# Two half terms of k side by side behind an up and a down pass

## The chip, the cores and the metric

The kernel runs on one core of one Trainium2 chip. The metric is the device time of one execution in microseconds (us), the median of several runs. All arithmetic is in float32.

## The reference, cut to what matters

A batch of 8 images with 512 channels and 32 x 32 positions goes through four layers, image by image except for the routing of the last:

```python
# layer 0: group norm, 8 heads of attention, three inner steps, projection, residual
q, k, v = split(qkv_w @ group_norm(x) + qkv_b)
h = softmax(q.T @ k / 8) @ v
for _ in range(3):
    h = h + 0.1 * tanh(inl_w @ h + inl_b)
x = x + proj_w @ h + proj_b
# layer 1: one attention over the 1024 positions, with 64 channels for q and k, residual
x = v1 @ softmax(q1.T @ k1).T + x
# layer 2: 12-tap filters, twice as fine along both axes, leaky relu, back to 32 x 32
x = down2(leaky_relu(up2(x + bias), 0.2) * sqrt(2))
# layer 3: per image, weights mixed from 8 experts by a router, 1x1, 3x3, 1x1, residual
w1, w2, w3 = (sum(gate[e] * w[e] for e in range(8)) for w in (W1, W2, W3))
out = relu(bn3(w3 @ relu(bn2(conv3x3(w2, relu(bn1(w1 @ x)))))) + x)
```

## The kernel before

Channels or positions lie on the 128 partitions of SBUF. Large products (q, k, v, inner steps, projection, and the weighting of layer 1) are done by Strassen's scheme in Winograd's form: seven half-sized products instead of eight, named P1, C11, U2, U3, C22, C21 and C12, and gathered by additions on VectorE as the PSUM banks are evacuated. Expert weights of layer 3 are mixed for seven images together (`blend_early`) and for the last one by itself.

The work is a loop over the 8 images: `layer0`, `layer1`, then `between` for images 0 to 6, or `last_across`, `last_rows` and `last_columns` for image 7, after which layer 3 of all images follows. `between(b)` holds layer 2 of image b together with q, k and v of image b + 1, so that TensorE has work while layer 2 waits for its evacuations and its trips through DRAM.

Layer 2 applies filters as small matmuls. `wide` filters along one axis, its result is written to DRAM (`across`) and read back turned (`turned`). Then come the vertical passes, in eight steps n (two halves e of the channels, four steps i each):

- `up(e, i)` (L1178): 8 matmuls, each shown as 2 records, in TensorE tiles of 32 x 64 (L1188), into two pairs of PSUM banks from `ps_sc`, which has just these two. ScalarE writes 0.2 times each pair to a tile `fine` (L1194), VectorE takes the maximum of the two (L1195).
- `down(e, i)` (L1197): 8 matmuls, shown as 16 records, in tiles of 64 x 32 (L1206) over `fine`, into two banks of `ps_tp`; two copies into a tile `sent` (L1212), on ScalarE, or one of them on VectorE in odd steps; four stores of `sent` to DRAM (`back_u`, L1215). `sent` has two buffers.
- `turn_back(e)` (L1219), after the fourth step of a half: two loads that bring the half back turned (L1224). After the passes `narrow` (L1226) filters what they bring.

`fine_passes` (L1260) writes the order out: round n issues up(n), a filling, down(n - 1) and another filling, for n from 0 to 8 (no down in round 0, no up in round 8). In images 0 to 6 one filling is the next of the 14 half terms of k, two halves of each of the seven products (`in_turn`, L577: 4 records of 128 x 128 matmuls at L607, in banks of `ps_mm`, which has two). Its evacuation is one instruction: on ScalarE for P1 and C11 (L624, L626), on VectorE for the others (L628, L635). In image 7 (`last_rows`, L1351) one filling is two of the 34 pieces of `blend_early` (L291): one matmul each (L297), a copy to a tile `mix` of four buffers, by ScalarE for odd and VectorE for even pieces (L301), and a store to DRAM from POOL's queue (L302). The third and sixth fillings also load the 2 MB of images 0 and 1 for layer 3 (`load_z`, L1382); after every seventh piece follows a load of further experts (L288).

Inside these parts TensorE, VectorE, ScalarE and SP run in the order of the program (`hand`, L1274: `tc.manual_schedule`); POOL's order is made by the scheduler. So is what crosses from one hand-written part to the next: SP has the first two loads of image 0's mixed weights (L1442) ahead of the last `turn_back`.

Of the kernel before, what the change touches and what calls it, by code (L numbers as in the profile page):

```python
# [54 lines left out]
def tile_sequence(ctx: ExitStack, tc: tile.TileContext, a: dict, out: bass.AP, shifted: bool):  # L55
# [1084 lines left out]
    class Layer2:  # L1140
# [119 lines left out]
        def fine_passes(self, fill=lambda: None):  # L1260
            order = [(e, i) for e in range(2) for i in range(4)]
            for n in range(len(order) + 1):
                if n < len(order):
                    self.up(*order[n])
                fill()
                if n:
                    e, i = order[n - 1]
                    self.down(e, i)
                    if i == 3:
                        self.turn_back(e)  # L1270
                fill()

    engines = mybir.EngineType
# [409 lines left out]
```

## Time and profile before

| what | value |
|---|---|
| median of 3 runs | 3649.24 us (3649.09 to 3654.0) |
| profiled execution, device time | 3648.9 us |
| its span, first to last instruction | 3647.0 us |
| granted TensorE clock | 0.998 of full speed |
| TensorE, VectorE, ScalarE busy | 3572.2, 2406.2, 1329.7 us |
| up passes, 1024 records (L1188) | 587 to 639 ns each, several at once |
| down passes, 1024 records (L1206) | 589 to 613 ns each, several at once |
| stores of mixed weights (L302), to landing | 3.0 / 6.4 / 10.0 us min / median / max |
| stores of `sent` (L1215), to landing | 2.3 us median |
| loads of `turn_back` (L1224), to landing | 7.6 us median |

Lines of the page group instructions by their line in the source, engine and tiles; "x" is a count. PE is TensorE's matmul, PEld its weight load, DVE is VectorE, ACT ScalarE, SP and POOL the engines whose queues issue the transfers (SPq, POOLq and so on are the queues themselves). The chain is the work that ended last, followed back from the end of the program. A wait reads "who waited <- for whom: us in total, times, longest". Where several matmuls run at the same time in different tiles, their records overlap, and only the distance from the start of one block to that of the next tells what the block costs.

### The profile page before, as it was taken

Reading aid. Unit: us, or ns where it says so; the run is one execution under the profiler, and the core shown is the slowest. Engines: PE = TensorE matmul, PEld = TensorE weight load, DVE = VectorE, ACT = ScalarE, POOL = GpSimd, SP = SyncE. Lnnn points to the kernel's source line nnn. Section 1 sums busy time; section 2 is a strip of 40 time slices with the busy share of each in tenths; the row PEclk is TensorE's granted clock in tenths of the full one; section 3 lists DMA queues with packets and bytes.
Section 4 is the critical chain, followed back from the end, with each engine's and each line's share of the span. In section 5 each row is a group of like instructions: output and inputs, shape, how many; then the busy total and the mean of one; then the engine's idle time right before and its main releaser. Section 6 shows DMA issues by size and latency. Waiting matters only on the chain.

```text
span 3647.0 us, 47655 instructions
## 1 busy us (share of the span) xinstructions
PE 3572.2 (98%) x19445; PEld 1751.4 (48%) x19445; DVE 2406.2 (66%) x3201; ACT 1329.7 (36%) x1772; POOL 102.0 (3%) x139
## 2 busy tenths in 40 slices
PE   8999999999999999999999999999999999999799
PEld 4346543474435643474435743465434744355243
DVE  4887568765777558765687658774687657765434
ACT  0632345223542246223452236323452235422343
POOL 4100000000000000000000000000000000001100
PEclk9999999999999999999999999999999999999999
DMA  5102440116101450015301351024401261015872
GB/s 200 50 1 84 130 162 1 45 65 198 69 1 64 133 179 1 32 53 170 122 1 64 97 174 42 1 84 130 162 1 46 66 201 64 1 43 190 311 272 108
DMA packets 139813, 348.24 MB, mean 95 GB/s; under 512 B 14720, under 2 KB 89488, under 8 KB 132800
## 3 DMA queue, kind: packets, MB, share of 16 engines
q1 hardware_dynamic: 135120, 325.96, 26.0%
q0 software_dynamic: 4320, 18.87, 1.4%
q8 instruction: 155, 2.54, 0.3%
q14 instruction: 74, 0.61, 0.1%
q10 hardware_dynamic: 144, 0.26, 0.0%
HBM read 226.55 MB, written 118.49 MB: 95 GB/s over the span
## 4 chain that ended last, share of the span: by engine, by line
PE 94%; DMA 2%; issue 1%; ACT 1%; DVE 1%; POOL 0%; SPq 0%; POOLq 0%; ACTq 0%; DVEq 0%
PE scores L827 12%; PE av L868 12%; PE inl_X L552 7%; PE inl_A L552 5%; PE av_X L1129 5%; PE inl_Y L552 5%; PE av_A L1129 3%; PE av_Y L1129 3%; PE v_X L552 3%; PE c L1497 2%; PE proj_X L552 2%; PE v_X L607 2%; PE k_X L607 2%; PE v_Y L552 2%; PE av L881 2%; PE q_X L607 2%
## 5 line engine op out<-in xcount | busy, mean ns | idle before, releaser
L846 ACT ACTIVATE e<-scores 128x1024 f32<-128x1024 f32 x504 | 516.6, 1025 | 434.4 <-PE scores L827 379.3
L827 PE MATMUL scores<-q,k 64*64 64x512 f32 x4096 | 531.9, 592 | 0.0
L868 PE MATMUL av<-e,v 64*64 64x512 f32 x4096 | 528.7, 589 | 0.0
L852 DVE TENSOR_TENSOR acc<-acc,e 128x1024 f32<-128x1024 f32 x320 | 389.3, 1217 | 37.4 <-ACT e L846 35.4
L868 PEld LDWEIGHTS av<-e,v 64*64 64x64 f32 x4096 | 156.6, 133 | 282.8 <-issue 276.8
L827 PEld LDWEIGHTS scores<-q,k 64*64 64x64 f32 x4096 | 150.4, 133 | 295.5 <-issue 220.8
L552 PE MATMUL inl_X<-T_hf,w_inl 128*128 128x512 f32 x576 | 261.6, 592 | 0.0
L1195 DVE TENSOR_TENSOR fine<-up,fine 128x1024 f32<-128x1024 f32 x128 | 150.8, 1220 | 118.8 <-ACT fine L1194 116.5
L889 DVE RECIPROCAL inv<-av 128x256 f32<-128x256 f32 x128 | 223.1, 1748 | 2.1 <-PE av L881 2.1
L692 ACT ACTIVATE inl_U<-inl_U,inl_b 128x512 f32<-128x512 f32 x96 | 66.8, 719 | 304.4 <-DVE inl_U L707 304.4
L552 PEld LDWEIGHTS inl_X<-T_hf,w_inl 128*128 128x128 f32 x576 | 108.8, 190 | 137.9 <-issue 111.7
L552 PE MATMUL inl_A<-hf,w_inl 128*128 128x512 f32 x384 | 174.6, 597 | 0.0
L1194 ACT ACTIVATE fine<-up 128x1024 f32<-128x1024 f32 x128 | 124.1, 1022 | 134.1 <-PE up L1188 121.1
L850 DVE TENSOR_TENSOR acc<-e,e 128x1024 f32<-128x1024 f32 x64 | 79.3, 1240 | 111.3 <-ACT e L846 92.3
L703 DVE TENSOR_TENSOR inl_U<-inl_X,inl_P 128x512 f32<-128x512 f32 x96 | 61.8, 685 | 109.9 <-PE inl_X L552 109.9
L1129 PE MATMUL av_A<-v,eT 128*128 128x256 f32 x512 | 122.6, 383 | 0.0
L552 PEld LDWEIGHTS inl_A<-hf,w_inl 128*128 128x128 f32 x384 | 71.5, 190 | 96.8 <-issue 86.3
L1129 PE MATMUL av_X<-v,eT 128*128 128x256 f32 x512 | 114.0, 381 | 0.0
L1016 ACT ACTIVATE eT<-scores 128x512 f32<-128x512 f32 x128 | 66.1, 602 | 115.4 <-PE scores L379 115.4
L1129 PEld LDWEIGHTS av_X<-v,eT 128*128 128x128 f32 x512 | 96.6, 190 | 19.3 <-DVE av_U L1103 6.5
L1166 ACT COPY wide<-wide 128x1024 f32<-128x1024 f32 x62 | 59.8, 1015 | 122.4 <-PE wide L1158 122.4
L1036 POOL TENSOR_TENSOR seen<-seen,acc 128x512 f32<-128x512 f32 x16 | 20.3, 1269 | 3006.6 <-DVE acc L1028 3006.0
(377 smaller groups left out, 5562.2 us busy)
## 6 DMA issues: line engine op xcount, KB each, us to landing
x<-in_x_dram SPq DMA_DIRECT2D x64, 512.0 KB, 9.3
across_u<-wide SPq DMA_DIRECT2D x128, 256.0 KB, 3.7
turned<-across_u SPq DMA_DIRECT2D x64, 512.0 KB, 5.9
back_u<-sent SPq DMA_DIRECT2D x256, 128.0 KB, 2.3
back<-back_u SPq DMA_DIRECT2D x32, 1024.0 KB, 7.6
w_v<-stored_u_v SPq DMA_DIRECT2D x14, 1792.0 KB, 7.4
out_dram<-z SPq DMA_DIRECT2D x31, 512.0 KB, 2.8
spill_u<-z SPq DMA_DIRECT2D x28, 512.0 KB, 5.9
```

The lines of the kernel that those rows point to most:

```text
L552: nc.tensor.matmul(dst, lhs, rhs, start=(opens and s == 0 and cc == 0), stop=(cc == 1 and s == rows), skip_group_check=True,)
L607: nc.tensor.matmul(dst, lhs, rhs, start=(what in opens and s == 0 and cc == 0), stop=(cc == 1 and s == rows), skip_group_check=True,)
L827: nc.tensor.matmul(ps[r][rows[c]], k[rows[r], oc, jc * P + c * HD : jc * P + c * HD + HD], q[rows[r], oc, ts(sh, HALF)], start=True, stop= ...
L846: nc.scalar.activation(e, pair, AF.Exp, scale=HD ** -0.5)
L850: nc.vector.tensor_add(accs[g], exps[t - 1], e)
L852: nc.vector.tensor_add(accs[g], accs[g], e)
L868: nc.tensor.matmul(avs[g][r][rows[c]], v[rows[r], jc, ts(2 * oc + c, HD)], e[rows[r], ts(c, HALF)], start=(jc == 0), stop=(jc == SC - 1),)
L881: nc.tensor.matmul(ps[rows[r]], ones[:, 0:HD], acc[:, ts(r, HALF)], start=True, stop=True)
L889: nc.vector.reciprocal(copies[g][:, at], totals[g][:, at])
L1129: nc.tensor.matmul(ps[:, ts(s, QR)], left[:, j, at : at + P], right[:, j, :], start=(what in ("P1", "U2", "C22") and s == 0 and j == 0), s ...
L1194: nc.scalar.mul(t, ps, 0.2)
L1195: nc.vector.tensor_max(t, ps, t)
```

## The change

In each round of `fine_passes` the first filling moves from before the down pass to behind it. Round n is then up(n), down(n - 1), with the turn back after every fourth step, and two fillings.

```diff
             for n in range(len(order) + 1):
                 if n < len(order):
                     self.up(*order[n])
-                fill()
                 if n:
                     e, i = order[n - 1]
                     self.down(e, i)
                     if i == 3:
                         self.turn_back(e)
+                fill()
                 fill()
```

No instruction is added or removed. In images 0 to 6 TensorE's queue in round 1 was up, C11, down, U3 and becomes up, down, C11, U3, and likewise in the rounds to 6; the copies of a down pass now stand ahead of both evacuations of k on ScalarE and VectorE. Rounds 0, 7 and 8 keep their order, since there is no down pass in the first and no half term left in the last two.

In image 7 the four pieces of a round follow the down pass together. The last two of the 34 pieces come in round 8, and so stand behind the last down pass instead of ahead of it. On SP the stores of down pass 0 go ahead of the load of image 0 (L1382), and those of down pass 2 ahead of the last load of experts (L288); all else keeps its place. On POOL the two stores change places within four pairs of pieces (4 and 5, 12 and 13, 20 and 21, 28 and 29).

## Prediction

> **What bounds the kernel now.** I read the page's busy row and chain first, to learn which engine's time is the kernel's time.
>
> ```profile
> PE 3572.2 (98%) x19445; PEld 1751.4 (48%) x19445; DVE 2406.2 (66%) x3201; ACT 1329.7 (36%) x1772; POOL 102.0 (3%) x139
> ...
> PE 94%; DMA 2%; issue 1%; ACT 1%; DVE 1%; POOL 0%; SPq 0%; POOLq 0%; ACTq 0%; DVEq 0%
> ```
>
> TensorE is busy for 98% of the span and carries 94% of the chain, so a microsecond taken out of its queue is a microsecond of the kernel, except where it waits. The change touches eight stretches: one per image. The chain in order of time for image 1 (start, length, what) shows such a stretch:
>
> ```profile
> 849.87 1.04 PE up L1188 x16
> 850.92 1.91 PE k_A L607 x4
> 852.83 1.72 PE k_X L607 x4
> 854.55 1.06 PE up L1188 x16
> 855.61 1.91 PE k_A L607 x4
> 857.52 1.02 PE dn L1206 x16
> 858.54 1.91 PE k_X L607 x4
> 860.46 1.04 PE up L1188 x16
> ...
> 889.92 1.04 PE up L1188 x16
> 890.96 1.11 PE dn L1206 x16
> 892.08 0.76 ACT fine L1194
> ```
>
> Three things are to be seen. There is no gap between up at 849.87 and up at 889.92: TensorE sets the pace. A half term of k costs 1.91 us directly behind an up or down pass, but 1.72 us behind another half term (850.92 and 852.83). And the last up is followed directly by a down pass, which begins 1.04 us after it, exactly as a half term does: the new neighbourhood already occurs once per image.
>
> The timeline gives the evacuation of the up pass (start, length, engine, what):
>
> ```profile
> 891.03 1.94 ACT L1194 ACTIVATE fine<-up 128x1024 f32<-128x1024 f32 x2 [2.31 <-PE up L1188]
> 892.09 2.36 DVE L1195 TENSOR_TENSOR fine<-up,fine 128x1024 f32<-128x1024 f32 x2 [1.38 <-ACT fine L1194]
> ```
>
> From up's start at 889.85 in that view to the end of the maximum at 892.09 + 2.36 = 894.45 it is 4.60 us; the next up can't begin earlier, since both pairs of PSUM banks are then taken.
>
> Image 7 differs: its filling is the mixing of the experts. The sums by stretch (second one) and its waits say what bounds it:
>
> ```profile
> 3342.00:3412.00 70.00, 51.77 (x324) 13.29 (x324) 31.55 (x37) 30.29 (x44) 17.89 (x34) 1.00 0.95 345
> ```
>
> ```profile
> ACT mix L301 <- DMA mixed_u<-mix: 22.5, 8, 3.8
> ...
> ACT sent L1212 <- DMA back_u<-sent: 7.8, 3, 3.4
> PE narrow L1237 <- DMA back<-back_u: 7.1, 2, 5.9
> ```
>
> The last two columns of the first are the DMA share and GB/s: 0.95 and 345. TensorE is busy 51.8 of 70 us there; the transfers are the bound.
>
> [...] Up works in 32x64 tiles, down in 64x32 and k in 128x128, [...] the trace agrees that seams cost (1.91 against 1.72), and prices up to down no higher than up to k (1.04 both). [...] the extra 0.19 us is the size of one 128x128 load (190 ns on the profile's page), which fits a load left bare at the seam, though nothing shows that it is the cause. [...]
>
> **The change, part by part.** Each call of the passes makes nine rounds.
>
> *Images 0 to 6, TensorE.* Before, rounds 1 to 6 are up, k, down, k: 1.04 + 1.91 + 1.02 + 1.91 = 5.88 us (in the chain 29.46 us for the five rounds from up at 860.46 to up at 889.92, 5.89 each). After, they are up, down, k, k: 1.04 + 1.02 + 1.91 + 1.72 = 5.69 us. The saving is 0.19 to 0.20 us a round; I take 0.195. Round 0 has no down pass and keeps its order. Rounds 7 and 8 have none of the 14 half terms left (2 + 6 x 2 = 14) and keep theirs. So 6 x 0.195 = 1.17 us an image, 7 x 1.17 = 8.2 us in all. Bounds: 42 x 0.19 = 8.0 and 42 x 0.20 = 8.4. After the passes come v and the next image's attention, where TensorE is again without gaps, so the time isn't given back.
>
> *What moves with a down pass, and its cover.* Each brings 8 matmuls (16 records), two copies of 0.59 to 0.69 us on ScalarE and VectorE, and four stores on SP; every fourth also the two loads of the turn back. (1) Down waits for the maximum of the up before: done at 4.60 us into a round, while the next up begins at 5.69: cover 1.09 us, before 1.29. It is needed by up anyway, so this adds no wait. (2) The copies now stand ahead of both k evacuations on ScalarE and VectorE, not between them. Per round VectorE has at most 2.36 + 0.68 + 0.75 + 0.75 = 4.54 us of work and ScalarE 1.94 + 1.18 + 0.69 = 3.81, both under 5.69. The first k of a round ends at 3.97 us; behind maximum and copy its evacuation ends near 4.60 + 0.68 + 0.75 = 6.0, 0.3 us into the next round, and the earliest half term that needs it or its bank starts 2.06 us in. Nothing, with 1.7 us to spare; if the cover went, the k behind would wait for the shortfall. (3) The stores leave earlier in their round; the two buffers of sent give each two rounds to land, now 11.4 instead of 11.8 us. The median landing is 2.3 us; only dn4's stores, queued behind a turn back of 7.6 us, come near. They cost nothing as long as sent6's copy, behind two activations in round 7, finishes before the maximum of up7 ends. I take 0; a microsecond late would cost up to 1 us an image, and is the upper bound's reason.
>
> *The end of the passes.* Up7, down6, down7 run as before, waiting for up7's evacuation; that stall of some 3.5 us an image stays.
>
> *Image 7.* After, a round is up, down, then four pieces of mixing. Seams save at most 0.2 us a round, and are hidden by the transfers: 0. SP: the stores of down 0 now precede the 2 MB load of z0, and those of down 2 precede the last experts' load; same bytes in the same queue, so what is queued behind all of them (down 3's stores, then the turn back, then down 4's) lands within about 0.5 us of before. POOL: within some pairs of pieces the stores swap places, 0.53 us each. ScalarE: the copies of a down pass stand ahead of both mixing copies. Where they wait for their buffer (7.8 us in three waits), two mixing copies and the next round's L1194 are queued behind them, instead of one. In round 7 that delays piece 29, and pieces 32 and 33 now follow down 7 on TensorE instead of preceding it. Down 7 itself is held by sent6, which waits for down 4's stores, so it stays near 3411. The first weights' load needs piece 32 and stands ahead of the turn back on SP: piece 32 is a down pass and a copy later, 1.02 + 0.69 = 1.7 us; I let 0.5 of it show, since the turn back waits for down 7's own stores anyway, which land some 6.8 us after down 7 begins (3411.13 to 3417.91). That is 0.5 us worse against about 0.5 better from the stores that go ahead: net 0. Bounds -3 (three waits on sent shortened to half) and +4 (piece 29 waits as long as the longest such wait, 3.8).
>
> *Sum.* Against the profiled execution (3648.9 us, span 3647.0 and 1.9 around it): 3648.9 - 8.2 + 0 = 3640.7. The median of the runs, 3649.24, is 0.3 higher: 3641.0.
>
> **The rivals.**
> A, forecast: seams saved, image 7 within its bounds of -3 and +4: 3638 to 3645. Chance 0.72.
> B, image 7's transfers also get better: the waits on sent (7.8 us) all go, because stores go ahead of 2 MB loads, and half of this reaches the end: 8.2 + 3.9 = 12.1, 3637.1. For it: those waits exist. Against: 0.95 DMA share. Chance 0.1.
> C, slower: in image 7 four mixing copies in a row must each find their buffer's last store landed. A store takes a median of 6.4 and up to 10.0 us; if the evacuation of up (4.6), the two mixing copies in ScalarE's queue and that landing run in series rather than beside each other, rounds grow from 8.2 to about 10 us, seven times 1.8 = 12.6, net +4.4: 3653.6. It decides from a growth of 8.2 / 7 = 1.2 us a round. Against: one buffer's loop, a landing plus about 1 us, already sets the round today. Chance 0.06, and 0.07 for a smaller growth that leaves 3645 to 3649.
> D, the change doesn't save: the seam from up to down costs more where k would have followed, or evacuation sets the round at 5.89: 3649. Against: the direct seam at 890.96 and 1.09 us of cover. Chance 0.05.
>
> **How the numbers follow.** The likeliest is A, 3641.0. Leaving out most of B's far side, C and D, 3637.5 to 3645.5 holds some 8 in 10. Changes under 0.2% (7.3 us, about what a measurement of this kernel can tell from none) count as the same: the border is 3641.9, inside A. A lies below it with 0.7 of its chance: 0.5, and B's 0.1: 0.6 faster. C's far part beyond 3656.5 gives 0.03 slower; the rest, 0.37, is the same.
>
> **What would show it.** Right: in the chain, up at 1.04, dn at 1.02, k at 1.91, k at 1.72, and 5.69 us from up to up in rounds 1 to 6; about 46.4 instead of 47.6 us from the first up to the first v of images 0 to 6; image 7's first up to its second narrow pass of half 1 unchanged within 4 us. Wrong: a wait of PE up on DVE fine, a k term waiting for L628 or L635, dn above 1.1 us behind up, or rounds of image 7 above 9 us.

## The result and the profile after

| | before | after |
|---|---|---|
| median of 9 runs each, side by side | 3652.08 us (3649.09 to 3656.84) | 3643.37 us (3639.71 to 3647.46) |
| profiled execution, device time | 3648.9 us | 3643.3 us |
| its span | 3647.0 us | 3641.3 us |
| first up to first narrow, images 0 to 6 | 46.49 us | 45.31 us |
| first narrow to the next image's scores | 32.65 us | 32.65 us |
| first up of image 7 to first product of layer 3 (`c`) | 91.7 us | 94.4 us |

The ratio is 0.9977, with an interval of 0.9967 to 0.9988: faster by 0.23%, just beyond the 0.2% that the prediction set as its border, with that border inside the interval. The forecast was 3641.0 us, the measurement 3643.37.

The page's busy row and chain of the kernel after. The chain is still TensorE's. Its busy time, with the same 19445 records, is only 1.8 us less: it fell by 8.4 us between the first up of image 0 and the first up of image 7, and rose by 7.3 us from there on, where image 7's stretches at a granted clock of 0.50 or 0.51 add up to 30.7 us instead of 10.2.

```profile
PE 3570.4 (98%) x19445; PEld 1757.2 (48%) x19445; DVE 2405.3 (66%) x3201; ACT 1325.9 (36%) x1772; POOL 101.9 (3%) x139
...
PE 95%; DMA 2%; issue 1%; ACT 1%; DVE 1%; POOL 0%; SPq 0%; POOLq 0%; DVEq 0%; ACTq 0%
```

The chain in order of time of the kernel after, image 1 (start, length, what):

```profile
853.08 1.06 PE up L1188 x16
854.14 1.02 PE dn L1206 x16
855.16 1.91 PE k_A L607 x4
857.08 1.72 PE k_X L607 x4
858.79 1.04 PE up L1188 x16
```

From up at 853.08 to up at 858.79 it is 5.71 us, where it was 5.91 (854.55 to 860.46); the rounds that follow take 5.69 or 5.70, without a gap. The second k costs 1.72 us. Six rounds and seven images of this are the whole gain: 7 x (46.49 - 45.31) = 8.3 us, beside 8.7 us between the medians, whose interval runs from 4 to 12 us. What follows the passes is not touched (32.65 us in both).

The end of the evacuation of up7, the last of image 1, in the timeline of the kernel after (start, length, engine, what):

```profile
889.44 2.35 DVE L1195 TENSOR_TENSOR fine<-up,fine 128x1024 f32<-128x1024 f32 x2 [1.39 <-ACT fine L1194]
```

Up7 starts at 887.20 there, so it is evacuated after 889.44 + 2.35 - 887.20 = 4.59 us, as before. In the six rounds ahead of it no matmul waits for an evacuation.

The weight loads of round 1 of image 1 in the same timeline (start, length, then, in brackets, the idle time of the weight loader) show where a seam lies:

```profile
855.09 0.30 PEld L607 LDWEIGHTS k_A<-x,w_k 128*128 128x128 f32 x2 [0.84 <-issue]
855.63 0.19 PEld L607 LDWEIGHTS k_A<-x,w_k 128*128 128x128 f32 x1 [0.24 <-issue]
...
857.77 0.19 PEld L607 LDWEIGHTS k_X<-T_h,w_k 128*128 128x128 f32 x1 [0.24 <-issue]
858.72 0.23 PEld L1188 LDWEIGHTS up<-turned,up_v 32*64 32x64 f32 x16 [0.76 <-issue]
```

Inside the pair a load follows the last by 0.43 us (856.06, 856.49, 856.92). Into the pair it takes 855.63 - 855.09 = 0.54, 0.11 more than 0.43, and out of it 858.72 - 857.77 = 0.95 for two matmuls, 0.09 more than twice 0.43. So a stay in 128x128 tiles costs about 0.11 going in and 0.09 coming out, 0.20 in all, with two k terms inside; before the change a round with two stays of one k term each took 5.91 us, 0.20 more than the 5.71 here. Of the two stays in a round one is left.

### The profile page after: what moved, and what is told of

It is laid out like the page before. It is cut to its first block, busy times and chain, and to the rows that moved or that the text cites. A ratio compares the mean times of both kernels' runs of the same rounds, so it can differ in the third digit from the quotient of the medians.

```text
span 3641.3 us, 47652 instructions
## 1 busy us (share of the span) xinstructions
PE 3570.4 (98%) x19445; PEld 1757.2 (48%) x19445; DVE 2405.3 (66%) x3201; ACT 1325.9 (36%) x1772; POOL 101.9 (3%) x139
## 4 chain that ended last, share of the span: by engine, by line
PE 95%; DMA 2%; issue 1%; ACT 1%; DVE 1%; POOL 0%; SPq 0%; POOLq 0%; DVEq 0%; ACTq 0%
PE scores L827 12%; PE av L868 12%; PE inl_X L552 7%; PE inl_A L552 5%; PE av_X L1129 5%; PE inl_Y L552 5%; PE av_A L1129 3%; PE av_Y L1129 3%; PE v_X L552 3%; PE c L1497 2%; PE proj_X L552 2%; PE v_X L607 2%; PE k_X L607 2%; PE v_Y L552 2%; PE av L881 2%; PE q_X L607 2%
```

## The experiments

All are compared with the kernel before, run beside them on the same chip. `fine_passes` gets an argument `split`: `True` is the order of before (up, k, down, k), and without it the order is that of the change.

**Images 0 to 6 alone, and image 7 alone.** The change touches two kinds of stretch; each was made without the other.

```diff
-            two.fine_passes(fill)                                # last_rows, image 7
+            two.fine_passes(fill, split=True)
```

> The new order in images 0 to 6 alone, the old one in image 7. Seam theory (a half term of k costs 0.19 us less behind another half term, and nothing in image 7 matters): from first up to first narrow pass 45.3 us in images 0 to 6, and 8.2 us less than before in all, a ratio of 0.9977 to 0.9978. Rival (the new order of image 7 costs something, which the gain of the seams hides: its first up to the first product of layer 3 took 94.4 us in the changed kernel and 91.7 before): this kernel is some 2.5 us faster than the changed kernel, about 11 us less than before, a ratio of 0.997.

```diff
-            two.fine_passes(lambda: next(parts, None))           # between, images 0 to 6
+            two.fine_passes(lambda: next(parts, None), split=True)
```

> The new order in image 7 alone, the old one in images 0 to 6. Seam theory: images 0 to 6 as before, 46.5 us from first up to first narrow pass, and a ratio of 1.000. Rival (image 7's order costs 2.7 us through the clock granted to TensorE): a ratio of 1.0007, and shares of the clock below 1.0 between the first up of image 7 and the first product of layer 3 which the kernel before doesn't show.

Measured: images 0 to 6 alone 3643.74 us, ratio 0.9977 (0.9968 to 0.9987), which is the whole change. Image 7 alone 3651.42 beside 3651.29, ratio 1.0001 (0.9992 to 1.0009). The gain is that of the seams. The medians show nothing given or taken by image 7, though their intervals leave room for some 3 us either way. The +2.7 us of image 7 in the table above can't be told from scatter: in the nine profiles of this study the same stretch takes 94.4 and 94.1 us in the changed order, and 91.5 to 95.4 in the old one.

**Two k terms ahead of down.** If only the number of stays counts, up, k, k, down must be as good as up, down, k, k. Images 0 to 6 take it (`split="late"`); image 7 keeps the old order. The cut shows what the argument does.

```diff
                     self.up(*order[n])
+                    fill()
+                    fill()
                 if n:
                     e, i = order[n - 1]
                     self.down(e, i)
                     if i == 3:
                         self.turn_back(e)
-                fill()
-                fill()
```

> In images 0 to 6 up, two half terms of k, then down; image 7 in the old order. It has as many seams as the changed kernel, but the down pass comes last in its round and next to the following up. Seam theory: the same 5.69 us a round and the same gain as with down behind up, 8.2 us, ratio 0.9977. Rival (the gain comes from down passes and their copies starting earlier, which gives evacuation and stores more time): no gain or less than half of it, ratio 0.999 to 1.000.

Measured: 3654.05 us, ratio 1.0009 (1.0003 to 1.0016), 10 us above the change. The expectation of the seams was missed. The chain in order of time of this kernel, image 1:

```profile
867.84 1.04 PE up L1188 x16
...
873.54 1.04 PE up L1188 x16
...
888.26 6.59 DMA back_u<-sent
...
895.00 0.59 ACT sent L1212
...
895.64 1.67 PE dn L1206 x16
...
897.97 2.06 PE narrow L1237 x16
900.03 3.71 PE v_A L607 x8
```

The rounds are what the seams promised: 5.70 us from up at 867.84 to up at 873.54. The loss comes behind them: the chain runs through a transfer of `sent`, 6.59 us long, to down 6's copy and only then to down 7. The timelines show the copy with its wait, first in this kernel, then in the kernel after:

```profile
895.00 1.07 ACT L1212 COPY sent<-dn 128x512 f32<-128x512 f32 x2 [1.32 <-DMA back_u<-sent]
```

```profile
890.21 1.08 ACT L1212 COPY sent<-dn 128x512 f32<-128x512 f32 x2
```

Down 6's copy needs the buffer of `sent` that down 4's stores empty. In the kernel after they land at 889.41, and ScalarE, which has not idled, comes to the copy 0.80 us later. (The chain there names a store of `sent` too, landed at 890.02; it is one of down 5's, whose buffer the copy of down 7 needs.) Here ScalarE waits for them 1.32 us. The way there, each time counted from the image's first up (848.40 after, 851.76 here):

| | after | up, k, k, down |
|---|---|---|
| down 3 begins | 22.8 us | 26.4 us |
| its first store is issued | 27.0 us | 28.4 us |
| first turn back is issued (SP) | 30.5 us | 31.9 us |
| its second load has landed | 39.7 us | 41.8 us |
| down 4's last store, behind it, has landed | 41.0 us | 43.1 us |
| ScalarE has done what stands ahead of down 6's copy | 41.9 us | 41.9 us |

Of the 3.6 us by which down 3 is later, 2.2 are absorbed, since its copy on VectorE no longer queues behind a maximum; 1.4 reach the turn back, 0.7 are added by the transfer, and down 4's stores, in the queue behind 2 MB, come too late. From down 6 to down 7 it is 2.61 us in five images of the kernel after, and 2.72 and 2.74 in images 5 and 6; here, image by image, 3.12, 4.04, 2.61, 3.53, 2.84, 3.50 and 2.68.

From the first up to the first narrow this makes at most 1.3 us an image (46.60 against 45.31), but the period from one image to the next grew by up to 3.8. The rest is in the last two lines of the chain. The chain of the kernel after has, in their place:

```profile
893.64 1.19 PE narrow L1237 x16
894.84 1.92 PE v_A L607 x8
```

So the narrow pass takes 2.06 instead of 1.19 us, and v_A 3.71 instead of 1.92. The sums by stretch of this kernel say why; the third column from the right is the granted clock of TensorE:

```profile
897.60:904.20 6.60, 6.23 (x32) 3.08 (x40) 2.14 (x4) 0.32 (x1) 0.00 (x0) 0.50 0.65 173
```

After the longer stall TensorE was granted half its clock (0.50) for 6.8 us; from 890.6 to 897.4 and from 904.4 to 907.0 it is 1.00. That happened in five of the seven images (from 474.3, 897.5, 1737.2, 2157.0 and 2576.9 us on). They are the five with the longest way from down 6 to down 7. Image 1 among them has a period of 422.3 us (418.5 in the kernel after), the other four have 420.5 to 421.3 (417.9); image 2, undisturbed, keeps the 417.92 of the kernel after.

**Down 3 early.** If the late turn back is the cause, it is enough to bring forward down 3 alone. Round 4 returns to the changed order, the other rounds stay up, k, k, down. The cut is shortened to the condition that changes.

```diff
-                if split == "late":
+                if split == "late" and n != 4:
                     fill()
                     fill()
```

> As two half terms of k ahead of down (images 0 to 6, image 7 old), but in round 4 down 3 stands directly behind up 4 again, so that the turn back of the first half starts 3.6 us earlier. Theory of the miss (down 3 last in its round puts the turn back's 2 MB later, the stores of down 4 land behind it, sent6's copy waits for that buffer, down 7 waits for the copy, and TensorE's longer pause lets its clock be halved): no wait of sent6 on a store, first up to first narrow pass 45.3 us in all images, no halved clock in images 0 to 6, ratio 0.9977. Rival (what harms is the down pass 5 standing next to up 7 and down 6, with less matmul work just ahead of the pause): halved clocks and a loss of 2 to 3 us an image stay, ratio 0.9995 to 1.001.

Measured: 3645.24 us, ratio 0.9986 (0.9978 to 0.9994): most of the 10 us is back, and the rival has fallen, though 0.9977 is not reached. In image 1 down 4's stores land at 891.05, and down 6's copy starts 0.85 us later (891.90). Down 6 to down 7 is 2.61 us in six images; in image 5 the copy still waits for the stores, it is 3.05, and the clock is halved (0.50) from 2567.3 us on. An undisturbed image is 0.28 us longer than in the kernel after (418.20 against 417.92), 7 x 0.28 = 2.0 us in all, and the chain in order of time, image 1, shows where:

```profile
870.57 1.02 PE dn L1206 x16
871.59 1.04 PE up L1188 x16
872.63 1.30 PE dn L1206 x16
```

Down 3 is now only one up pass behind down 2. The copies that free down 2's banks start at 871.72, the second of them ends near 872.8 on ScalarE, and down 3 waits for it: 1.30 instead of 1.02.

**Filling the stall.** The prediction left the stall behind up7 as it is. Four half terms of v, which the kernel has next anyway, are put into rounds 7 and 8 of images 0 to 6: with the changed order, with up, k, k, down in rounds 1 to 6, and with the old order. Image 7 keeps the old order in all three.

```diff
+            ahead = []
+
+            def fill():                       # k while there is any, then v
+                if next(parts, True) is None:
+                    return
+                if not ahead:
+                    ahead.extend(values(b + 1, x, t, w))
+                next(ahead[1])
+
-            two.fine_passes(lambda: next(parts, None))
-            all_of(parts)
+            two.fine_passes(fill)
...
-            v, parts = values(b + 1, x, t, w)
+            v, parts = ahead
...
-            steps[4:4] = [None] * 3
+            steps[4:4] = [None] * 2
```

> The new order in images 0 to 6 (image 7 old), and rounds 7 and 8, which have no half term of k left, filled with the first four half terms of v; two of the pauses ahead of the second half's narrow passes kept so that its transfer has as long to land. Theory (the 3.4 us between up7 and the first narrow pass that TensorE waits for the last evacuation are free for other work, and the chain of image 0 to 6 is TensorE's alone): 3.4 us less an image, 0 to 0.4 of it lost to seams between v and the passes, 21 to 24 us in all beyond the new order, ratio about 0.9915. Rival (the stall moves on: the turned-back second half lands too late, or v's banks are taken): narrow waits for back by 1 to 3 us an image, ratio 0.995 to 0.9975.

> Two half terms of k ahead of down in rounds 1 to 6, and four half terms of v behind down 6 and down 7. Theory of the miss: sent6's copy still waits for the stores of down 4, but v keeps TensorE busy for 3.65 us meanwhile, so that neither a pause nor a halved clock follows in images 0 to 6, and the whole is as fast as down behind up with v in the stall: 3620 to 3624 us, ratio 0.9915 to 0.992. Rival (the order itself costs): 2 to 3 us an image more than that, ratio 0.996 to 0.9975.

> The old order of the rounds (one half term of k behind each pass) with four half terms of v behind down 6 and down 7. If seams and stall are independent: 8.2 us more than with the new order and v in the stall, some 3630 us, ratio 0.994. Rival (part of the gain of the new order came from starting the stall's copies and stores earlier, which no longer counts when the stall is filled): less than 4 us more, ratio 0.9928 or lower.

| order in images 0 to 6, with v in the stall | median | ratio | period of an image |
|---|---|---|---|
| up, down, k, k | 3621.83 us | 0.9918 (0.9905 to 0.9932) | 414.85 us |
| up, k, k, down | 3621.01 us | 0.9917 (0.9903 to 0.993) | 414.84 us |
| up, k, down, k | 3631.62 us | 0.9948 (0.9934 to 0.9961) | 416.36 us |

The chain in order of time of the first of them, at the end of image 1's passes:

```profile
885.30 1.04 PE up L1188 x16
886.35 1.02 PE dn L1206 x16
887.37 1.92 PE v_A L607 x8
889.29 1.73 PE v_X L607 x8
891.02 1.02 PE dn L1206 x16
...
895.69 1.02 PE narrow L1237 x16
```

TensorE doesn't stop any more; a down pass takes 1.02 where down 6 and 7 took 2.61 and 2.79. Each image is 417.92 - 414.85 = 3.07 us shorter than in the kernel after. None of the 21 images has a halved clock; in image 1 of the first of them it is 1.00 from 886 to 907 us. With the stall filled, the order that lost 10 us alone is level with the change. In image 1 its copy of down 6 still waits for the stores (total, times, longest, from 882 to 897 us):

```profile
ACT sent L1212 <- DMA back_u<-sent: 1.2, 1, 1.2
```

The wait is there, in six of the seven images and for up to 1.7 us, but TensorE has v to do meanwhile: it is the stall behind the wait that made the order lose. All three expectations held, the last with 9.8 us for 8.2, and none of their rivals did. The old order is 9.8 us slower than the first row, against 8.3 without v. Its chain shows why it is more:

```profile
886.37 1.04 PE up L1188 x16
887.41 1.92 PE v_A L607 x8
889.33 1.02 PE dn L1206 x16
890.35 1.93 PE v_X L607 x8
892.28 1.86 PE v_A L607 x8
...
897.08 1.02 PE narrow L1237 x16
```

From up to narrow it is 897.08 - 886.37 = 10.71 us here and 895.69 - 885.30 = 10.39 there, 0.32 more. Some 0.19 of it is a seam: the four half terms of v make three stays between the small tiles here and two there. The other 0.13 is a wait: v_A at 892.28 takes 1.86 us instead of 1.73, since its first load is held until VectorE has read out the v_A before it (L665), as the timeline has it:

```profile
892.14 1.59 PEld L607 LDWEIGHTS v_A<-w_v,x 128*128 128x128 f32 x8 [0.27 <-DVE v_P1+_0_4855 L665]
```

With 1.18 us from the k terms that makes 1.50 an image; the periods differ by 1.51, in all 7 x 1.51 = 10.6 us. The two best kernels, 3621.83 and 3621.01 us, beat both kernels of this case by 0.6 to 0.8%, and their intervals don't tell them apart.

## Why the prediction was right

- **The seams.** 0.195 us a round, 1.17 an image and 8.2 in all were forecast; 0.197, 1.18 and 8.3 were measured, and the change in images 0 to 6 alone gives the whole ratio. The neighbourhood of up and down, read at the end of each image's passes before the change, held in all rounds. Of the reason given, one load left bare at the seam (0.19 us in the trace), only the size holds: the trace divides the 0.20 between the way in (0.11) and the way out (0.09). What it is made of was not shown by any run here.
- **The first up to the first narrow** shortened by 1.18 us, as forecast. The forecast wrote 46.4 instead of 47.6 to the first v, which begins one narrow pass later; in the chain after that is 894.84 - 848.40 = 46.4.
- **Cover (1), the maximum of up, and cover (2), the copies ahead of k.** Both held: no matmul of rounds 0 to 6 waits for an evacuation. The experiment with down 3 early found the neighbouring limit, which the prediction didn't name: the banks of down itself, which are free only some 2.3 us after the down pass before began.
- **Cover (3), down 4's stores.** The prediction named the right place and condition, and gave it no number. From the landing to down 6's copy it is 0.8 to 1.4 us in images 0 to 4 of the kernel after (0.80 in image 1). In images 5 and 6 nothing is left: the copy starts 0.14 and 0.10 us after the landing, and down 7 comes 0.1 us late. Before the change it was 0.1 to 1.5 us, so the order did not use the margin up; that the term came out near 0 was partly luck all the same, as the kernel with the change in images 0 to 6 alone shows. In its image 5 the copy waited, down 7 came 0.35 us late, the clock was halved (0.50), and the image lost 2.7 us. With down 3 late the margin is gone in six of seven images. In the passes this costs 0.5 to 1.3 us in the five images, about the "up to 1 us an image" of the prediction; but a halved clock (0.50) follows, and an image loses 2.6 to 3.8 us in all. The bound lacked that part.
- **Image 7.** A net of 0 was forecast, and the run with image 7 alone gives 0 (1.0001). The terms under it can't be confirmed one by one, so the 0 is in part luck. A wait of the kernel after from 3330 to 3415 us (total, times, longest):

```profile
ACT sent L1212 <- DMA back_u<-sent: 1.5, 1, 1.5
```

This wait of ScalarE was 7.8 us before, and rival B said that it would go. But it is 2.4 us in the run with image 7 alone, and in the seven profiles with the old order in image 7 it is anything from nothing to 7.8 (1.0 with the change in images 0 to 6 alone), so the fall isn't shown to come from the order. The time did not follow it, and B fell. The transfers kept nearly their rate in the first 70 us from image 7's first up: 0.93 and 339 GB/s, beside 0.95 and 345 before.

```profile
3333.50:3403.50 70.00, 57.40 (x323) 14.96 (x324) 32.01 (x37) 30.59 (x44) 16.92 (x32) 0.88 0.93 339
```

Rival C needed rounds longer by 1.2 us; their mean is 8.6 and 8.4 us in the two profiles with the new order, and 8.1 to 8.5 in the seven with the old (8.2 before). D fell with the seams. From image 7's first up to its second narrow pass of half 1 it is 88.2 us instead of 86.5, within the 4 us allowed. The last stores landed 9.8 us behind down 7 instead of 6.8, where the prediction allowed 0.5 us. In the run with image 7 alone that was 6.4 us, and in the old order it is 6.2 to 7.5, so whether the 9.8 belongs to the order stays open.
- **The base.** The forecast is lower than the measurement by 2.4 us though its saving was only 0.5 us smaller than the difference of the medians: it was set against a median of three runs, 3649.24 us, and nine give 3652.08. The profiled execution before had the clock at 0.998, while the 37 runs of that kernel beside the first experiments had 0.994 to 0.997, with 3648.08 to 3655.2 us: the six slowest all at 0.994 or 0.995. The term that was off is the start of the sum, not the change.

## What to carry to other kernels

Count how often TensorE changes between small tiles and 128x128 tiles, and put blocks of the same tiling side by side: the price was 0.20 us a stay here, and the profile shows it in blocks of the same kind with two lengths (k at 1.91 and 1.72). Before a step is moved, follow its stores and loads to the next wait on the same queue and give the margin a number: two orders with the same seams differed by 10 us by when one turn back was issued. Where a stall is left beside the edit, fill it first, since work of 7 us that had to be done anyway saved 3.1 us an image and took away the sensitivity to the place of the down pass, though not to the number of seams.

## What the runs showed of the hardware

- In the six kernels that leave the stall empty, seven of the 42 images show a granted clock of 0.50 after the stall, and they are those with 2.84 us or more from down 6 to down 7; the other 35 have 2.61 to 2.74. Five are in the kernel with two k terms ahead of down, one in that with down 3 early, and one in that with the change in images 0 to 6 alone (2.96 us, 0.50 from 2564.4 to 2571.2), where the copy of down 6 waited for down 4's stores too. What sets the clock was not shown.
- A longer wait at down 7 cost more than itself: under a clock of 0.50 the narrow pass took 2.06 us instead of 1.19 and v_A 3.71 instead of 1.92 (image 1, two k terms ahead of down). The granted clock of the whole execution is 0.991 to 0.994 in the 21 runs of that kernel, and 0.994 to 0.996 in the nine of the kernel after.
- With the change in images 0 to 6 alone, image 5 lost 2.7 us (a period of 420.66 instead of 417.92) where down 7 came 0.35 us late, beside a spread of some 7 us between the runs of one kernel. In image 7, where TensorE waits for transfers, the profile before has one stretch at 0.50 (10.2 us, from 3422.5 on) and the profile after has five at 0.50 or 0.51 (30.7 us in all, between 3332.8 and 3428.4). That such stretches make that spread is an estimate: it fits the clocks of 0.994 and 0.995 in the six slowest runs above, but was not tested by itself.
